# Two graph layers on one core: no idle products at the start, layer 0's last norm behind the first turned blocks of layer 1, and another order at the end

## The chip, the cores and the metric

The kernel runs on one core of a Trainium2 chip. The metric is the device time of one execution in microseconds (us). Engines are named as the profile does: PE is TensorE's products, PEld its weight loads, DVE is VectorE, ACT is ScalarE, POOL is GpSimd, SP is SyncE, which here only issues DMAs.

## What is computed

`x` is 4096 x 512 in float32 and `adj` 4096 x 4096 in int32, with some 0.8% of ones. Two layers follow each other:

```
# layer 0
keep    = (adj > 0) & (cumsum(adj > 0, axis=1) <= 64)
nb_mean = (keep @ x) / max(keep.sum(1), 1)
xj      = leaky_relu(nb_mean @ W_nb.T + b_nb)          # slope 0.01
xi      = leaky_relu(x @ W_line.T + b_line)
x1      = layernorm(x + xi + where(cnt > 0, xj, 0))
# layer 1
Wh  = x1 @ W + bW
e   = leaky_relu((Wh @ a1 + b1)[:, None] + (Wh @ a2 + b2)[None, :], slope 0.2)
att = softmax(where(adj > 0, e, -9e15), axis=1)
out = layernorm(x1 + att @ Wh)
```

## The kernel before

The 4096 rows are 32 blocks of 128. The order of instructions on each engine is the order in which the program writes them: no scheduler moves anything, so an engine that waits holds up all that is written after it on that engine. The same holds for the DMAs that one engine issues. Tiles come from pools with a fixed number of buffers; a tile that takes over a buffer waits for the last reader of the tile before. The pools of layer 1 lie over memory that layer 0 used, and wait for its last readers in the same way.

**Start (L382 to L394).** W_nb and W_line are loaded, brought into order by a VectorE copy, transposed by TensorE in four parts each (`turn_w`, `turn_by_pe`, L149, L282) and copied from PSUM by ScalarE (L150). `spin(n)` puts n transposes of an identity matrix, which nobody reads, on TensorE: 12 at the start and 2 ahead of each part of W_nb. `fold_w` (L356) multiplies W with a1 and a2 on VectorE.

**Layer 0, first stage.** For each block, two products with W_nb and W_line (L340); y = x W_nb^T is split into `y_hi` and `y_lo`. Beside it, adjacency rows are loaded (L160), thresholded by ScalarE (L167), scanned by VectorE for the limit of 64 neighbours (L179 to L184) and stored as byte codes in DRAM (`code_d`).

**Layer 0, second stage.** For each block i, four groups g of 16 products (L502) sum y over its neighbours. Behind group g, `finish(i - 1, g)` does a quarter of the block before: g = 0 scales and bends (L462, L465), g = 1 adds the block's own part, loaded from `own_d` (L497), and takes the statistics (L469, L117 to L123; the power is POOL's), g = 2 applies the norm (L128) and stores the row in `x1_d` (L476), g = 3 takes two dot products with the rows `wa_row` (L481). After the loop, block 31 is finished by itself.

**Layer 1, first product (L786).** For each of 32 strips s of x1: `load_turned(s)` loads it in four DMAs on SP (L553) into one of four slots of `x1s`, `turn_x1(s)` transposes it on VectorE (L566) into a tile `c` of a pool of two, and four products with W make Wh. `finish_wh(s)` (L575) adds the bias row `bias_w` (tile `res`, loaded on SP at L538) into `bt`, and for each second half also makes four differences of it (L580 to L583), so that the later products need seven instead of eight per pair (Winograd's form of Strassen's scheme). At strips 8 to 15, `mask` (ACT L604, then DVE L607) and `score` (ACT L596) of the first two blocks' weights stand in the same loop, `greatest` and `shift` take the row maximum, and at strips 12 to 19 `weigh` (ACT L649) takes the exponential. At strips 22 and 26, `turn` (L668) and `combine` (L681 to L684) prepare the first two parts of the weights.

The terms e2 and st that the masks and scores need go through DRAM on POOL's queue (L763 to L771), behind layer 0's last block.

**Layer 1, weighted sums (L707).** 16 pairs of blocks, each in four parts k; `consume` makes seven products of each part into four PSUM banks: `where` puts products 1 and 2 into one bank, 4 and 7, 5 and 6 into one each, and 3 by itself. Sums of a pair are put together by `end_low` and `end_top` (L732 to L743) and finished by `end_row` (L748, norm, store L752), during the next pair; for the last pair all of this comes after the loop:

```
order = (1, 2, 4, 7, 5, 6, 3) if q < NP * NT - 1 else (1, 2, 6, 7, 5, 4, 3)
...
end_weights(NT - 1)
end_low(NT - 1)
end_row(NB - 1, nc.scalar)
end_top(NT - 1)
end_row(NB - 2, nc.sync)
```

## Time and profile before

| | us |
|---|---|
| median of 3 runs | 1620.12 |
| the 3 runs | 1619.28 to 1620.49 |
| the profiled execution, time | 1619.29 |
| the profiled execution, span | 1617.5 |
| mean granted TensorE clock in it | 0.996 |

The profile is of one execution, and all its clock times count from the span's start. Its time is 1.79 us more than its span, which is what lies around the span. A line of the timeline gives the start, the duration, the engine, the line of the program, the instruction and its tiles; in brackets stands how long the engine stood idle before it and what ended the idling. The trace lists each float32 product twice, so one strip of L786, which is four products, stands there as x8.

### The profile page before, as it was taken

The numbers are of one execution on the slowest core, as the hardware profiler recorded it, in microseconds if no ns is written. First come the engines' busy times: TensorE is split into PE (matmuls) and PEld (weight loads), VectorE is DVE, ScalarE is ACT, GpSimd is POOL, SyncE is SP. The second block draws the span as 40 slices with busy tenths as digits, with TensorE's granted clock in tenths as the row PEclk, the third lists the DMA queues.
The fourth block names the chain that finished last, engine by engine and source line by source line (L and its number), as shares of the span: only waits on it lengthen the run. The fifth ranks groups of instructions, "written<-read, shape, count | busy, mean of one in ns | idle before, by whom it ended". The sixth has DMA issues, their size and how long they took to land.

```text
span 1617.5 us, 18487 instructions
## 1 busy us (share of the span) xinstructions
PE 1584.3 (98%) x6456; PEld 1220.1 (75%) x6456; DVE 1328.7 (82%) x2183; ACT 902.5 (56%) x1054; POOL 257.7 (16%) x395
## 2 busy tenths in 40 slices
PE   9999999999999999989899999999999999999997
PEld 5444448888888787854358888888888888888886
DVE  4999987999999999847787778788888788788763
ACT  2655556677676766413337555567555567555520
POOL 4455532222222221120000000000000000000000
PEclk9999999999999999999999999999999999999999
DMA  8887878767776876352311111111111111111100
GB/s 194 282 260 240 260 210 241 217 196 210 220 212 194 217 205 187 92 130 79 92 46 27 53 40 53 40 27 53 53 40 53 40 28 52 53 40 53 40 7 33
DMA packets 168205, 192.74 MB, mean 119 GB/s; under 512 B 101376, under 2 KB 134176, under 8 KB 159920
## 3 DMA queue, kind: packets, MB, share of 16 engines
q1 hardware_dynamic: 147968, 131.51, 30.1%
q0 software_dynamic: 19712, 59.27, 10.7%
q8 instruction: 50, 0.82, 0.2%
q10 hardware_dynamic: 432, 0.79, 0.1%
q14 instruction: 43, 0.35, 0.1%
HBM read 132.65 MB, written 42.08 MB: 108 GB/s over the span
## 4 chain that ended last, share of the span: by engine, by line
PE 70%; DVE 20%; DMA 4%; issue 3%; ACT 2%; POOL 1%; SPq 0%; POOLq 0%; DVEq 0%; ACTq 0%
PE acc L707 34%; PE pt L707 14%; PE acc L340 9%; PE acc L502 9%; DVE left L179 8%; PE acc L786 4%; DVE left L184 2%; DVE junk L481 2%; DMA a<-in_adj_dram 1%; DVE st L117 1%; DVE own L469 1%; DMA late<-in_x_dram 1%; DVE t L465 1%; DVE t L462 1%; POOL rs L123 1%
## 5 line engine op out<-in xcount | busy, mean ns | idle before, releaser
L502 PE MATMUL acc<-y_hi,kt 128*128 128x512 f32 x1016 | 396.0, 390 | 3.1 <-ACT kt L249 3.1
L502 PE MATMUL acc<-y_lo,kt 128*128 128x512 f32 x1016 | 395.3, 389 | 0.0
L707 PE MATMUL acc<-bt,s 128*128 128x256 f32 x1536 | 342.3, 379 | 0.0
L707 PEld LDWEIGHTS acc<-bt,s 128*128 128x128 f32 x1536 | 291.8, 190 | 39.7
L604 ACT ACTIVATE w<-nat,far 128x1024 f32<-128x1024 uint8 x128 | 136.9, 1135 | 291.6 <-DVE a L668 238.9
L123 POOL TENSOR_TENSOR rs<-ve,neg_half 128x1 f32<-128x1 f32 x64 | 76.0, 1187 | 1026.5 <-DVE ve L121 1026.5
L707 PE MATMUL acc<-bt,a 128*128 128x256 f32 x1024 | 231.6, 379 | 0.0
L707 PE MATMUL pt<-bt,a 128*128 128x256 f32 x1024 | 231.5, 379 | 0.0
L502 PEld LDWEIGHTS acc<-y_hi,kt 128*128 128x128 f32 x1016 | 190.7, 188 | 44.9 <-ACT kt L249 5.3
L502 PEld LDWEIGHTS acc<-y_lo,kt 128*128 128x128 f32 x1016 | 190.7, 188 | 39.4
L707 PEld LDWEIGHTS pt<-bt,a 128*128 128x128 f32 x1024 | 194.6, 190 | 26.9 <-issue 0.5
L707 PEld LDWEIGHTS acc<-bt,a 128*128 128x128 f32 x1024 | 194.6, 190 | 26.5
L668 DVE STREAM_TRANSPOSE a<-w 128x1024 f32<-128x1024 f32 x128 | 153.0, 1225 | 59.4 <-ACT w L649 52.7
L167 ACT ACTIVATE edge<-a,steep 128x2048 bf16<-128x2048 int32 x64 | 127.9, 1998 | 104.5 <-DVE left L184 82.4
L249 ACT ACTIVATE kt<-ktb,steep 128x1024 fp32r<-128x1024 uint8 x124 | 139.4, 1147 | 82.0 <-PE acc L502 64.9
L596 ACT ACTIVATE w<-w,st_n 128x1024 f32<-128x1024 f32 x128 | 149.4, 1233 | 50.7 <-DVE m L607 50.7
L607 DVE CUSTOM_DVE_ANT_0 w<-e_n,w 128x1024 f32<-128x1024 f32 x128 | 149.5, 1221 | 4.3 <-ACT w L604 2.9
L649 ACT ACTIVATE w<-w,nm 128x1024 f32<-128x1024 f32 x128 | 145.4, 1137 | 11.3 <-DVE nm L640 11.3
L179 DVE TENSOR_TENSOR_SCAN left<-two,edge 128x2048 bf16<-128x2048 f32 x32 | 141.3, 4417 | 12.0 <-ACT edge L167 10.9
L179 DVE TENSOR_TENSOR_SCAN left<-two,ends,edge 128x2048 bf16<-128x2048 f32 x32 | 143.2, 4476 | 0.0
L786 PE MATMUL acc<-w,c 128*128 128x512 f32 x256 | 113.6, 602 | 14.9 <-DVE c L566 14.9
L202 ACT CAST code<-left 128x2048 uint8<-128x2048 bf16 x64 | 120.6, 1884 | 7.6 <-DVE left L184 7.6
(114 smaller groups left out, 1529.3 us busy)
## 6 DMA issues: line engine op xcount, KB each, us to landing
a<-in_adj_dram SPq DMA_DIRECT2D x64, 1024.0 KB, 6.0
code_d<-code POOLq DMA_DIRECT2D x64, 256.0 KB, 5.3
nat<-code_d SPq DMA_DIRECT2D x256, 64.0 KB, 2.0
own_d<-xb POOLq DMA_DIRECT2D x32, 256.0 KB, 6.0
own<-own_d SPq DMA_DIRECT2D x32, 256.0 KB, 2.7
x_d<-own POOLq DMA_DIRECT2D x32, 256.0 KB, 2.6
w<-x_d SPq DMA_DIRECT2D x128, 64.0 KB, 2.0
res<-x_d SPq DMA_DIRECT2D x32, 256.0 KB, 2.8
```

What stands on the lines that cost most here:

```text
L167: nc.scalar.activation(edge_of[s], loaded.pop(s), AF.Sigmoid, bias=steep[:, 0:1], scale=STEEP, accum_out=cnts[:, h, b : b + 1],)
L179: nc.vector.tensor_tensor_scan(left, two.to_broadcast([P, CH]), e, NEIGHBORS + 2.0 if h == 0 else end, ALU.max, ALU.subtract,)
L249: nc.scalar.activation(kts[s], bytes_.rearrange("p t (i r) -> p t r i", r=2), AF.Sigmoid, bias=steep[:, 1:2], scale=STEEP,)
L340: nc.tensor.matmul(pl, lhs_t[:, k, :], w_t[name][:, k, :], start=(k == 0), stop=(k == NC - 1),)
L502: nc.tensor.matmul(accs[i], kt[:, k // 2, k % 2, :], term[:, j, :], start=(j == 0 and term is y_hi), stop=(j == NB - 1 and term is y_lo),)
L596: nc.scalar.activation(dst, src, AF.Prelu, bias=bias, scale=scale, alpha=0.2)
L604: nc.scalar.activation(w_i, nats[b, i // 2].bitcast(U8)[:, i % 2, :], AF.Relu, bias=far, scale=-FAR)
L607: nc.vector.tensor_tensor_reduce(w_i, e2_n, w_i, 1.0, -3e38, ALU.subtract, ALU.max, m4s[b][:, i : i + 1])
L649: nc.scalar.activation(w_i, w_i, AF.Exp, bias=nms[b][:, i : i + 1], accum_out=z4s[g][:, r, i : i + 1])
L668: nc.vector.transpose(a[:, r].rearrange("p s (i a) -> p i s a", a=SQ), wts[2 * g + r][:, :, ts(k, 8 * SQ)].rearrange("p i (s x) -> p i s x ...
L707: nc.tensor.matmul(banks[g][n], lhs[:, j, :], bt[:, 4 * k + j, rhs, :], start=(k == 0 and j == 0 and n == mate[0]), stop=(k == NP - 1 and ...
L786: nc.tensor.matmul(pws[s], x1t[:, m, :], ws[:, m, :], start=(m == 0), stop=(m == NC - 1))
```

## The change

- The two identity transposes ahead of each part of W_nb are left out. The 12 at the start stay.
- `late` (three rows: `wa_row` and `bias_nb`, and before them the loaded strips of x) becomes three tiles of a pool `rows` of three buffers, which stays open for layer 1. The turned strips of x1 from the fourth on, `top` and `low`, and the residual rows of even blocks come from `rows` too; the pools `c` and the second `res` buffer go. Five small constants become one tile.
- The second tile of the pool `l1_w`, `early`, is taken right after `front`. The first three turned strips, block 31's own row and its scratch tiles lie in it, and later the first block's weights.
- Block 31's four finishing steps move from the end of layer 0 behind the loads of strips 0 to 3, the load of its own row, the loads for the first masks, and the turns of strips 0 to 2 with the loads of strips 4 to 6. In the loop, strip s + 3 is turned where s + 2 was, and s + 7 loaded.
- The four differences of `bt` are taken from `finish_wh` into `combine_wh`, which is called for one set at a time from strip 16 on, except at 22 and 26, and for what is left in the first part of the weighted sums.
- In the last part the products come in the order 4, 1, 2, 6, 7, 5, 3, and the last pair's sums and norms are written out: the upper block is scaled and its statistics taken in two halves, and it is stored in two halves on two queues.

```diff
-            turn_w("nb", 2)
+            turn_w("nb")
...
+    rows = ctx.enter_context(tc.tile_pool(name="rows", bufs=3, reuse_waits="tile"))
+    late = [rows.tile([P, C], F32, name="c") for _ in range(3)]
+    wa_rows, bias_nb = late[0:2], late[2]
...
-                nc.gpsimd.dma_start(
-                    wa_row.rearrange("p k c -> p (k c)"),
-                    wa_d.rearrange("k c -> (k c)").partition_broadcast(P),
-                )
+                for k in range(2):
+                    nc.gpsimd.dma_start(wa_rows[k], wa_d[k].partition_broadcast(P))
...
+        spare = []
+        def place(name, bufs=2):
+            if spare:
+                return spare.pop(0)
+            return work.tile([P, C], F32, name=name, bufs=bufs)
...
             if g == 2:
-                owns[i] = work.tile([P, C], F32, name="own")
-                nc.sync.dma_start(owns[i], own_d[i])
+                if i < NB - 1:
+                    owns[i] = place("own")
+                    nc.sync.dma_start(owns[i], own_d[i])
...
-        for g in range(NS):
-            finish(NB - 1, g)
...
     front = wp.tile([P, NI, NS * SQ], F32, name="w")
+    early = wp.tile([P, NI, NS * SQ], F32, name="w")
+    spare += [early[:, i, C:] for i in (0, 2, 3)]
+    owns[NB - 1] = early[:, 1, C:]
...
-    bias_w = ep.tile([P, C], F32, name="res")
+    bias_w = ep.tile([P, C], F32, name="res", bufs=1)
     nc.sync.dma_start(bias_w, b_w.partition_broadcast(P))
...
     def turn_x1(s):
         if s < NS:
-            x1ts[s] = ep.tile([P, C], F32, name="c").rearrange("p (m i) -> p m i", i=P)
+            t = early[:, s, :C] if s < 3 else rows.tile([P, C], F32, name="c")
+            x1ts[s] = t.rearrange("p (m i) -> p m i", i=P)
...
         if h == 1:
+            later.append(kk)
+    later = []
+    def combine_wh():
+        if later:
+            b = bt[:, later.pop(0)]
             nc.vector.tensor_tensor(b[:, 4], b[:, 1], b[:, 0], ALU.subtract)
             nc.vector.tensor_tensor(b[:, 5], b[:, 3], b[:, 4], ALU.subtract)
             nc.vector.tensor_tensor(b[:, 6], b[:, 5], b[:, 2], ALU.subtract)
             nc.vector.tensor_tensor(b[:, 1], b[:, 3], b[:, 1], ALU.subtract)
...
-            wts[b] = wp.tile([P, NI, NS * SQ], F32, name="w")
+            wts[b] = early if b == 0 else wp.tile([P, NI, NS * SQ], F32, name="w")
...
-        order = (1, 2, 4, 7, 5, 6, 3) if q < NP * NT - 1 else (1, 2, 6, 7, 5, 4, 3)
+        order = (1, 2, 4, 7, 5, 6, 3) if q < NP * NT - 1 else (4, 1, 2, 6, 7, 5, 3)
...
-            x1rows[b] = ep.tile([P, C], F32, name="res")
+            if b % 2:
+                x1rows[b] = ep.tile([P, C], F32, name="res", bufs=1)
+            else:
+                x1rows[b] = rows.tile([P, C], F32, name="c")
...
+    for s in range(4):
+        load_turned(s)
+    nc.sync.dma_start(owns[NB - 1], own_d[NB - 1])
+    load_nat(0, 0)
+    load_nat(0, 1)
+    for s in range(3):
+        turn_x1(s)
+        load_turned(s + 4)
+    for g in range(4):
+        finish(NB - 1, g)
...
-    for s in range(4):
-        load_turned(s)
-    load_nat(0, 0)
-    load_nat(0, 1)
-    turn_x1(0)
-    turn_x1(1)
     for s in range(NS):
-        if s > 0:
-            load_turned(s + 3)
...
-        turn_x1(s + 2)
+        turn_x1(s + 3)
+        load_turned(s + 7)
...
+        elif s >= FIRST + 8:
+            combine_wh()
...
+        while q == 0 and later:
+            combine_wh()
...
+        if q == NP * NT - 1:
+            end_weights(g)
...
-    end_weights(NT - 1)
-    end_low(NT - 1)
-    end_row(NB - 1, nc.scalar)
-    end_top(NT - 1)
-    end_row(NB - 2, nc.sync)
+    p, rz = banks[NT - 1], rzs[NT - 1]
+    top, low = (rows.tile([P, 2, HC], F32, name="c") for _ in range(2))
+    x_top, x_low = x1rows[NB - 2].rearrange("p (h c) -> p h c", h=2), x1rows[NB - 1]
+    stt = nc.vector.scalar_tensor_tensor
+    st = stat.tile([P, 2, nc.vector.BN_STATS_DIM], F32, name="st2", bufs=1)
+    nc.scalar.copy(top[:, 0], p[1])
+    tt(top[:, 1], top[:, 0], p[6], ALU.add)
+    tt(top[:, 0], top[:, 0], p[2], ALU.add)
+    tt(low[:, 0], top[:, 1], p[7], ALU.add)
+    stt(top[:, 0], top[:, 0], rz[:, 0:1], x_top[:, 0], ALU.mult, ALU.add)
+    nc.vector.bn_stats(st[:, 0], top[:, 0])
+    tt(low[:, 1], low[:, 0], p[5], ALU.add)
+    tt(low[:, 0], low[:, 0], p[4], ALU.subtract)
+    y_low = low.rearrange("p h c -> p (h c)")
+    stt(y_low, y_low, rz[:, 1:2], x_low, ALU.mult, ALU.add)
+    low_stats = ln_stats(y_low)
+    tt(top[:, 1], top[:, 1], p[5], ALU.add)
+    stt(top[:, 1], top[:, 1], rz[:, 0:1], x_top[:, 1], ALU.mult, ALU.add)
+    stt(top[:, 1], p[3], rz[:, 0:1], top[:, 1], ALU.mult, ALU.add)
+    nc.vector.bn_stats(st[:, 1], top[:, 1])
+    mv, rs = ln_rs(st)
+    ln_apply(y_low, low_stats)
+    nc.scalar.dma_start(out_blk(NB - 1), y_low)
+    for h in range(2):
+        ln_apply(top[:, h], (mv, rs))
+        (nc.sync, nc.scalar)[h].dma_start(out_blk(NB - 2)[:, ts(h, HC)], top[:, h])
```

## The prediction, made before the changed kernel ran

> **What bounds the kernel now.** The page's table of engines first: TensorE is busy nearly throughout, so an edit elsewhere counts only where TensorE stands still.
>
> ```profile
> PE 1584.3 (98%) x6456; PEld 1220.1 (75%) x6456; DVE 1328.7 (82%) x2183; ACT 902.5 (56%) x1054; POOL 257.7 (16%) x395
> ```
>
> Then TensorE's own waits (columns: total us, times, longest):
>
> ```profile
> PE acc L786 <- DVE c L566: 14.9, 8, 7.7
> PE acc L502 <- ACT kt L249: 3.1, 4, 1.8
> PE acc L340 <- DVE xt L294: 1.8, 2, 1.0
> ```
>
> The waits for L566, the turned x1 blocks of layer 1's first product (L786), are three quarters of what TensorE loses inside the span. In the chain of waits L707 stands without a break from 834 to 1605 us, so what is won or lost before 834 us reaches the end. TensorE's timeline shows where the 14.9 us lie:
>
> ```profile
> 705.27 0.39 PE L502 MATMUL acc<-y_lo,kt 128*128 128x512 f32 x1
> 713.38 53.33 PE L786 MATMUL acc<-w,c 128*128 128x512 f32 x120 [7.72 <-DVE c L566]
> 768.28 3.70 PE L786 MATMUL acc<-w,c 128*128 128x512 f32 x8 [1.58 <-DVE c L566]
> 772.95 3.70 PE L786 MATMUL acc<-w,c 128*128 128x512 f32 x8 [0.97 <-DVE c L566]
> 777.66 3.70 PE L786 MATMUL acc<-w,c 128*128 128x512 f32 x8 [1.01 <-DVE c L566]
> 782.37 3.70 PE L786 MATMUL acc<-w,c 128*128 128x512 f32 x8 [1.01 <-DVE c L566]
> 786.72 20.87 PE L786 MATMUL acc<-w,c 128*128 128x512 f32 x48 [0.65 <-DVE c L566]
> 809.36 14.00 PE L786 MATMUL acc<-w,c 128*128 128x512 f32 x32 [1.77 <-DVE c L566]
> ```
>
> 7.7 us lie at the seam of the layers, the rest in products 15 to 29 of 32. An undisturbed product takes 3.43 us (VectorE's turns of x1, released by its end, are 3.43 us apart from 718.67 to 722.11); each restart costs some 0.1 us more. The seam in SyncE's timeline:
>
> ```profile
> 705.46 0.35 SPq L538 DMA_DIRECT2D res<-in_L_gnn_bW_dram  x1
> 705.86 7.74 SPq L553 DMA_DIRECT2D w<-x_d  x16
> 713.64 6.12 SPq L591 DMA_DIRECT2D nat<-code_d  x8
> ```
>
> Everything on SyncE's queue stands behind the load of bias_w (`res`), which waits for the last product on y_hi at 705.4. The x1 loads therefore start at 705.86, one per 0.46 us. Later the loop between ScalarE and VectorE sets the pace:
>
> ```profile
> 767.68 1.13 ACT L604 ACTIVATE w<-nat,far 128x1024 f32<-128x1024 uint8 x1
> 770.12 1.24 ACT L596 ACTIVATE w<-w,st_n 128x1024 f32<-128x1024 f32 x1 [1.30 <-DVE m L607]
> 771.26 1.13 ACT L649 ACTIVATE w<-w,nm 128x1024 f32<-128x1024 f32 x1
> 772.39 1.13 ACT L604 ACTIVATE w<-nat,far 128x1024 f32<-128x1024 uint8 x1
> ```
>
> L604, VectorE's L607 (1.23 us), L596, L649, L604 again: 772.39 − 767.68 = 4.71 us a round, against 3.43 for a product. The clock (the number after the five busy times) in half-microsecond stretches:
>
> ```profile
> 709.00:709.50 0.50, 0.00 (x0) 0.00 (x0) 0.10 (x1) 0.00 (x0) 0.25 (x1) 1.00 0.60 174
> 712.00:712.50 0.50, 0.00 (x0) 0.00 (x0) 0.46 (x4) 0.06 (x1) 0.00 (x0) 0.50 1.01 329
> 717.00:717.50 0.50, 0.50 (x2) 0.19 (x1) 0.00 (x0) 0.00 (x0) 0.00 (x0) 1.00 0.48 58
> ```
>
> It is 0.50 from 709.7 to 716.5. Last, the tail:
>
> ```profile
> 1604.30 0.42 DVE L733 TENSOR_TENSOR c<-c,acc 128x256 f32<-128x256 f32 x1 [17.76 <-PE acc L707]
> 1613.70 0.55 DVE L128 TENSOR_SCALAR c<-c,mv,rs 128x512 f32<-128x512 f32 x1 [0.73 <-POOL rs L123]
> 1614.28 0.34 SPq L752 DMA_DIRECT2D out_dram<-c  x1
> ```
>
> **The change part by part.** The sum is made against the profiled execution: 1617.5 us of span and 1.79 around it, 1619.29, which is 0.83 below the median of 1620.12 and at the fast end of the runs.
>
> **1. Spins between the parts of W_nb.** Eight identity transposes of 0.21 us go: 1.7 us of TensorE's queue, up to 1.3 us at the first L340 product (11.26). VectorE's copy (0.43) and ScalarE's (0.59) both fit under a part's four slow transposes (0.87), so TensorE stays busy from 4.8 to about 9.1 anyway. [...] The row: transposes were 0.21 us apart up to 9.75 and 0.13 us after. By the row alone the gain is 1.3 us; [...] Neither reaches the end: TensorE waits for VectorE's turned x again at 56.67 (0.75 us) and 85.48 (1.04 us), and VectorE is there behind the first adjacency load, issued at 24.75 after the fold of the attention vectors, which waits for the row a1 landing at 18.34. I enter 0; [...]
>
> **2. The seam.** The three turns now precede the norm of block 31 as if the products could follow layer 0 without a gap. They cannot. `early` lies in the third buffer, over y_hi's first blocks, and `res` still waits for the last y_hi product and still stands ahead of the x1 loads. The turns wait for loads that start at 705.86 as before. Their fourth pieces are issued at 707.3, 709.2 and 711.1 and, at the 2.7, 2.2 and 2.3 us to landing of these very issues in the trace, land at 710.0, 711.4 and 713.4. With 0.71 us a turn the first product starts at 710.8 instead of 713.38, and the third turn ends at 714.1. Three products take it to 721.1 at full clock.
>
> What pays is the norm, queued behind these turns. It starts at 714.1 instead of 705.70; its two first steps end at 715.6; its `own` row is now issued on SyncE after 16 x1 loads, at 713.64, and lands 2.7 us later (the median of that load) at 716.4. From there the old steps from 707.21 to 712.62 follow, 5.4 us: 721.9, then the fourth turn, 722.6. So product 3 cannot start before 722.65. On POOL, block 31's row and the loads of e2_n and st_n go 9.4 us later: the last of them, issued at 724.4 and 4.6 us under way (median), comes at 738.5 instead of 729. Score 8 asks for it at about 745.5. Covered by 7 us.
>
> The clock: the first product took 713.38 to 718.5, 5.1 us, as half of it ran at 0.50; 1.6 us lost. If the clock is 0.50 until 716.5 again, a product started at 710.8 loses 2.85 and product 3 starts at 723.95. [...] I take 723.3, between the two. Before it was 725.3 (718.5 and two products). Gain 2.0 us.
>
> **3. Look-ahead and late combinations.** The turned blocks have three buffers instead of two, and turn s+3 is made where turn s+2 was; the four subtractions on `bt` (1.58 us) leave products 5 to 16, one set following each product from 16 on, except at 22 and 26. Up to the shift at product 12 the ScalarE/VectorE loop just runs 2.0 us earlier: nm at 763.2 instead of 765.25. It keeps its 4.71 us, and part of the subtractions was hidden in it. What changes is which block each round turns. Turn 16 ends at 764.5 and 17, 18, 19 follow at 769.2, 773.9, 778.7 (before: 15 to 18 at 768.2, 772.9, 777.6, 782.3). TensorE wants 15 to 19 at 764.5, 767.9, 771.4, 774.8 and 778.2: one wait of 0.5 us instead of four. Product 20 needs turn 20, which comes after greatest (1.64), the lm and nm steps (1.35), one set of subtractions (1.58), one eviction (0.60) and itself (0.70): 784.6, a wait of 2.4. Before, product 20 started at 786.72 + 3.54 = 790.2. Gain 5.6 us, the 2.0 included.
>
> From there VectorE needs 0.60 + 0.63 + 1.58 = 2.8 us a product against 3.43, and gains on TensorE except at 22 and 26, where turning and combining a weight part takes 5.0: product 30 may wait 0.5 us. The end is 784.6 + 12 × 3.43 + 0.5 + 0.3 for restarts = 826.6, instead of 834.0. Gain 7.4 us in all.
>
> The last two sets come in the first weights part. VectorE, free at about 831, then has four masks (4.6), greatest to nm (3.1), two sets (3.2), and a turn with its combination (5.5): 847.4. The third part of products needs it at 826.6 + 24.2 = 850.8. 3.4 us to spare: L707 stays without a gap.
>
> **4. The tail.** The order 4, 1, 2, 6, 7, 5, 3 closes the bank of 4 and 7 before that of 5 and 6. VectorE's first sum waits for the latter: 5 ends one product (1.73 us) later than before, so the sum starts at 1604.30 + 1.73 = 1606.0. From there I add steps at their old pitch (0.34 to 0.48 for 256 elements; 256-element forms of the scaled sum and of the statistics, not in the trace, at 0.48, the 512 form less the 0.27 between L681 and L733): last statistics aggregated at 1612.9, with POOL's 0.9 the first half is scaled at 1613.8 and the second is issued at 1614.35. Before: 1614.28. Two transfers of half the size on two queues may land sooner; bounds −0.6 (two waits on POOL to one and a shorter transfer) to +0.4 (three transfers in flight). I take −0.2, near the equal issue times.
>
> **5. The rest.** `late`, x1's turned blocks, top, low and half of the residual rows share one pool of three; a residual row waits for the same read as before (the row step of the pair before), 36 us ahead of use. One more broadcast on POOL (0.55 us) falls in its idle time. 0.
>
> Sum: 7.4 + 0.2 = 7.6, 1619.29 − 7.6 = **1611.7 us**. Against the median the gain would be 8.4: its other runs lost up to 1 us more, perhaps to the clock at the seam.
>
> **The rivals.**
> A. Only the seam gains. If the third buffer comes free no earlier, or the ScalarE/VectorE loop itself must end before product 20, products 15 to 20 keep their waits. For: the loop keeps its 4.71 us. Against: turn 15 now stands ahead of the round that delayed it. 2.0 + 0.2: 1617.1 us. Chance 0.11.
> B. More than I count: the clock is never halved at the seam, TensorE's waits at 56.67 and 85.48 do not eat part 1, and the tail wins 0.6. For: the spread of the runs. Against: part 1's adjacency chain. 0.7 + 1.3 + 0.4 on top: 1609.3. Chance 0.12.
> C. Slower. The norm of block 31 is late, and e2_n and st_n wait behind it: their small pieces meet the x1 loads on the DMA engines (landing took 4.1 to 7.2 us at 713 to 726). Mask and score 8 hold all later turns. Free up to 7 us, then a microsecond each; slower than before from 15. At 20 us: 1611.7 + 13 = 1624.7. Against: twice the longest landing would still be covered. Chance 0.04.
>
> **How the numbers follow.** My forecast has 0.73. About 0.2% (3.2 us) is what a measurement here can tell from no change. Faster is the forecast and B, and a sliver of A: 0.86; same is the rest of A, 0.10; slower is C, 0.04. The forecast's own range is 1610 to 1614: −1 for the clock and the tail, +2 for restarts and DMA waits I did not see. For 8 in 10 I go from 1609.2, near B, to 1615.6, short of A.
>
> **What would show it.** TensorE's gap at the seam near 5.1 us, not 7.7 and not 0; the fourth turn at about 722; no wait at products 15 to 18, one of 2 to 3 us at product 20; the first weights product at 826 to 827; L707 without gaps; the last output as long after TensorE's end as before. The prediction is wrong if the seam's gap closes fully, if products 15 to 18 still wait, or if L707 shows waits in its first three parts.

## The result and the profile after

The changed kernel takes 1612.62 us (median of 6 runs, 1611.52 to 1614.06) beside 1620.3 us before (6 runs, 1619.28 to 1622.26): a ratio of 0.9951, 95% interval 0.9938 to 0.9964, 7.7 us less by the medians and about 7.9 by the ratio. The forecast was 1611.7. The profiled execution took 1612.2 us, with a span of 1610.4; all numbers of "after" below are from it.

In the changed kernel L509 is what L502 was (layer 0's products), L809 is L786 (layer 1's first product), L575 turn_x1, L724 is L707 (the products by the weights).

The page's table of engines: TensorE is as busy as before, in a span 7.1 us shorter.

```profile
PE 1583.4 (98%) x6448; PEld 1219.1 (76%) x6448; DVE 1328.3 (82%) x2186; ACT 903.2 (56%) x1054; POOL 258.2 (16%) x396
```

TensorE's waits (total us, times, longest): those for the turned x1 blocks were 14.9 us in 8 places and are 8.0 in 3. The block of the seam now carries the name `w`, as the first three turned blocks lie in `early`.

```profile
PE acc L809 <- DVE w L575: 5.4, 1, 5.4
PE acc L509 <- ACT kt L249: 2.9, 4, 1.8
PE acc L809 <- DVE c L575: 2.6, 2, 2.2
PE acc L340 <- DVE xt L294: 1.7, 2, 1.1
```

The same places in TensorE's timeline (start, duration, instructions, idle time before in brackets):

```profile
704.41 0.39 PE L509 MATMUL acc<-y_lo,kt 128*128 128x512 f32 x1
710.20 13.47 PE L809 MATMUL acc<-w 128*128 128x512 f32 x24 [5.40 <-DVE w L575]
723.51 55.10 PE L809 MATMUL acc<-w,c 128*128 128x512 f32 x128
778.95 3.70 PE L809 MATMUL acc<-w,c 128*128 128x512 f32 x8 [0.34 <-DVE c L575]
784.88 41.88 PE L809 MATMUL acc<-w,c 128*128 128x512 f32 x96 [2.23 <-DVE c L575]
826.60 3.62 PE L724 MATMUL pt<-bt,a 128*128 128x256 f32 x16
```

The seam's gap is 5.4 us. Products 0 to 2 take 13.3 us (710.20 to 723.51) where three undisturbed ones take 10.3. Products 3 to 18 run through; 19 waits 0.34 us, 20 waits 2.23, and after it nothing. The weights stage starts at 826.60 instead of 833.96.

SyncE's queue at the seam: the load of bias_w still stands ahead of the x1 loads and still goes out only when layer 0 ends; the `own` row of block 31 now comes behind 16 x1 loads.

```profile
704.61 0.35 SPq L546 DMA_DIRECT2D res<-in_L_gnn_bW_dram  x1
705.00 7.56 SPq L561 DMA_DIRECT2D w<-x_d  x16
712.65 0.38 SPq L777 DMA_DIRECT2D w<-own_d  x1
```

The clock (the number after the five busy times) in half-microseconds:

```profile
709.00:709.50 0.50, 0.00 (x0) 0.00 (x0) 0.06 (x1) 0.00 (x0) 0.00 (x0) 0.74 0.43 123
715.50:716.00 0.50, 0.50 (x2) 0.32 (x1) 0.37 (x1) 0.00 (x0) 0.00 (x0) 0.50 0.65 201
716.00:716.50 0.50, 0.50 (x2) 0.19 (x1) 0.47 (x2) 0.00 (x0) 0.00 (x0) 0.93 0.42 135
```

By the shares of the first and the last of these rows it falls at 709.2 and comes back at 716.1, so products 0 to 2 run 5.9 of their 13.3 us at half speed. And the tail: first sum, the upper row's statistics put together, POOL's `rs`, the two halves scaled, last issue.

```profile
1598.67 0.42 DVE L877 TENSOR_TENSOR c<-c,acc 128x256 f32<-128x256 f32 x1 [19.48 <-PE acc L724]
1605.37 0.21 DVE L122 BATCH_NORM_AGGREGATE mv<-st 128x2 f32<-128x12 f32 x1
1605.91 0.71 POOL L126 TENSOR_TENSOR rs<-ve,few 128x1 f32<-128x1 f32 x1 [1.76 <-DVE ve L124]
1606.66 0.74 DVE L131 TENSOR_SCALAR c<-c,mv,rs 128x256 f32<-128x256 f32 x2 [0.44 <-POOL rs L126]
1607.42 0.35 ACTq L896 DMA_DIRECT2D out_dram<-c  x1
```

TensorE ends at 1600.31; the last output is issued 7.11 us later (before: 6.62), and the span ends 10.09 us later (before: 9.84).

### The profile page after: what moved, and what is told of

The parts are those of the page before. It is cut to its first block, busy times and chain, and to the rows that moved or that the text cites. A ratio compares the mean times of both kernels' runs of the same rounds, so it can differ in the third digit from the quotient of the medians.

```text
span 1610.4 us, 18487 instructions
## 1 busy us (share of the span) xinstructions
PE 1583.4 (98%) x6448; PEld 1219.1 (76%) x6448; DVE 1328.3 (82%) x2186; ACT 903.2 (56%) x1054; POOL 258.2 (16%) x396
## 4 chain that ended last, share of the span: by engine, by line
PE 69%; DVE 23%; DMA 3%; issue 2%; ACT 1%; POOL 1%; SPq 0%; DVEq 0%; POOLq 0%; ACTq 0%
PE acc L724 34%; PE pt L724 14%; DVE left L179 10%; PE acc L340 9%; PE acc L509 9%; PE acc L809 3%; DVE left L184 2%; DVE junk L487 2%; DVE own L475 1%; DVE st L117 1%; DVE t L471 1%; DMA a<-in_adj_dram 1%; DVE t L468 1%; DVE own L131 1%; DVE c L575 1%
## 5 line engine op out<-in xcount | busy, mean ns | idle before, releaser
L509 PE MATMUL acc<-y_hi,kt 128*128 128x512 f32 x1016 | 395.8, 390 | 2.9 <-ACT kt L249 2.9
L509 PE MATMUL acc<-y_lo,kt 128*128 128x512 f32 x1016 | 395.3, 389 | 0.0
L724 PE MATMUL acc<-bt,s 128*128 128x256 f32 x1536 | 342.1, 379 | 0.0
L724 PEld LDWEIGHTS acc<-bt,s 128*128 128x128 f32 x1536 | 291.8, 190 | 39.7
L621 ACT ACTIVATE w<-nat,few 128x1024 f32<-128x1024 uint8 x128 | 136.9, 1135 | 277.1 <-DVE a L685 237.0
L126 POOL TENSOR_TENSOR rs<-ve,few 128x1 f32<-128x1 f32 x64 | 76.1, 1190 | 1020.5 <-DVE ve L124 1020.5
L724 PE MATMUL acc<-bt,a 128*128 128x256 f32 x1024 | 231.6, 379 | 0.0
L724 PE MATMUL pt<-bt,a 128*128 128x256 f32 x1024 | 231.5, 379 | 0.0
L509 PEld LDWEIGHTS acc<-y_hi,kt 128*128 128x128 f32 x1016 | 190.7, 188 | 44.4 <-ACT kt L249 4.8
L509 PEld LDWEIGHTS acc<-y_lo,kt 128*128 128x128 f32 x1016 | 190.7, 188 | 39.5
L724 PEld LDWEIGHTS pt<-bt,a 128*128 128x128 f32 x1024 | 194.6, 190 | 26.9 <-issue 0.5
L724 PEld LDWEIGHTS acc<-bt,a 128*128 128x128 f32 x1024 | 194.6, 190 | 26.5
L249 ACT ACTIVATE kt<-ktb,few 128x1024 fp32r<-128x1024 uint8 x124 | 139.8, 1147 | 84.7 <-PE acc L509 67.8
L167 ACT ACTIVATE edge<-a,few 128x2048 bf16<-128x2048 int32 x64 | 127.9, 1998 | 100.5 <-DVE left L184 78.3
L624 DVE CUSTOM_DVE_ANT_0 w<-e_n,w 128x1024 f32<-128x1024 f32 x128 | 149.5, 1221 | 9.1 <-ACT w L621 7.7
L179 DVE TENSOR_TENSOR_SCAN left<-few,edge 128x2048 bf16<-128x2048 f32 x32 | 141.3, 4417 | 12.4 <-ACT edge L167 11.3
L179 DVE TENSOR_TENSOR_SCAN left<-few,ends,edge 128x2048 bf16<-128x2048 f32 x32 | 143.2, 4476 | 0.0
L340 PE MATMUL acc<-wt_nb,xt 128*128 128x512 f32 x256 | 115.5, 594 | 2.5 <-DVE xt L294 1.7
```

Source lines behind the costliest of these rows:

```text
L167: nc.scalar.activation(edge_of[s], loaded.pop(s), AF.Sigmoid, bias=steep[:, 0:1], scale=STEEP, accum_out=cnts[:, h, b : b + 1],)
L179: nc.vector.tensor_tensor_scan(left, two.to_broadcast([P, CH]), e, NEIGHBORS + 2.0 if h == 0 else end, ALU.max, ALU.subtract,)
L249: nc.scalar.activation(kts[s], bytes_.rearrange("p t (i r) -> p t r i", r=2), AF.Sigmoid, bias=steep[:, 1:2], scale=STEEP,)
L340: nc.tensor.matmul(pl, lhs_t[:, k, :], w_t[name][:, k, :], start=(k == 0), stop=(k == NC - 1),)
L509: nc.tensor.matmul(accs[i], kt[:, k // 2, k % 2, :], term[:, j, :], start=(j == 0 and term is y_hi), stop=(j == NB - 1 and term is y_lo),)
L621: nc.scalar.activation(w_i, nats[b, i // 2].bitcast(U8)[:, i % 2, :], AF.Relu, bias=far, scale=-FAR)
```

## The experiments

Layer 0's last product ended at anything from 704.8 to 708.8 us in the fourteen traces of this study, with code ahead of it that differs in the spins and in where some tiles lie. A stretch that starts there is therefore a cleaner measure of the seam and of layer 1's first products than a total. The table has two stretches: from the end of layer 0 to the first product by the weights, and the part of it from product 3 on. (The trace of before merges products 0 to 14; product 3 is put at 725.4 there, as in the prediction.) Each is read from one trace. From product 3 on, kernels with the same loop agree within 0.1 us (103.1 or 103.2 in five), apart from m_warm; from layer 0's end to product 3 the seven traces with the changed seam scatter from 17.9 to 18.7 us. The ratio is to the kernel before, run on the same chip alongside it, with its 95% interval. Where an edit adds lines, the line numbers of that kernel's rows are a few off from the changed kernel's.

| kernel | layer 0's end | end to weights stage, us | product 3 to weights stage, us | ratio of times |
|---|---|---|---|---|
| before | 705.66 | 128.3 | 108.6 | 1 |
| changed | 704.80 | 121.8 | 103.1 | 0.9951 [0.9938, 0.9964] |
| a_spins | 705.98 | 128.5 | - | 0.9998 [0.9990, 1.0006] |
| b_old_tail | 705.66 | 121.1 | 103.1 | 0.9947 [0.9935, 0.9960] |
| c_early_sets | 707.47 | 121.1 | 102.7 | 0.9947 [0.9935, 0.9960] |
| d_ahead_2 | 704.93 | 121.8 | 103.8 | 0.9958 [0.9944, 0.9972] |
| h_seam_only | 706.01 | 123.7 | 105.8 | 0.9965 [0.9952, 0.9977] |
| n_two_bufs | 707.72 | 127.1 | 108.6 | 0.9979 [0.9973, 0.9986] |
| m_warm | 708.78 | 122.5 | 104.4 | 0.9954 [0.9941, 0.9968] |
| o_warm_20 | 707.40 | 122.0 | 103.1 | 0.9952 [0.9938, 0.9966] |
| e_bias_behind | 706.10 | 114.4 | 103.2 | 0.9904 [0.9889, 0.9918] |
| f_bias_slot | 706.89 | 114.1 | 103.2 | 0.9905 [0.9890, 0.9919] |
| k_mask_first | 706.23 | 118.8 | 100.2 | 0.9924 [0.9909, 0.9939] |
| l_all | 704.88 | 110.4 | 100.2 | 0.9878 [0.9864, 0.9891] |

### a_spins: the spins alone

```diff
-            turn_w("nb", 2)
+            turn_w("nb")
```

(in the kernel before, as the change has it)

> The kernel before with one edit of the change alone: no spins between the parts of W_nb. What is open: in the changed kernel's trace the last product of layer 0 ended 0.86 us earlier than before (704.8 against 705.66), which the prediction did not have. Theory (the prediction's part 1): the spins' time is eaten by the next wait for the turned x, the seam comes at 705.7 as before, the total is that of before within 0.3 us (ratio 1.0000). Rival (the spins are worth their time): the first L340 product comes at 10.5 instead of 11.3, layer 0 ends about 0.9 us earlier and the total falls by 0.9 us (ratio 0.9994).

Measured: no difference (1620.36 us beside 1620.40). The trace of this run shows why a gain of 0.8 us at the first product is not to be had for certain. TensorE's timeline, this kernel first, then the changed one:

```profile
5.29 4.70 PE L149 MATMUL pt<-ident,t 128*128 128x128 f32 x20 [1.10 <-DVE t L282]
10.67 5.42 PE L340 MATMUL acc<-wt_nb,xt 128*128 128x512 f32 x8 [0.68 <-ACT wt_nb L150]
```
```profile
5.28 4.53 PE L149 MATMUL pt<-ident,t 128*128 128x128 f32 x20 [1.09 <-DVE t L282]
10.49 3.70 PE L340 MATMUL acc<-wt_nb,xt 128*128 128x512 f32 x8 [0.68 <-ACT wt_nb L150]
```

The first four products of L340 (x8) come at 10.67 and 10.49 instead of 11.26, but here they take 5.42 us where they take 3.70 in the other. Of the thirteen traces of kernels without the spins, three (a_spins, f_bias_slot, k_mask_first) show 5.4 to 5.6 us at this place, ten 3.70. So the 0.6 to 0.8 us gained at the first product in these two (0.4 to 1.9 over the thirteen, beside the one trace with spins) are paid back in about one execution of four. And the 0.86 us by which layer 0 ended earlier in the changed kernel's profile is not shown to be a gain of the spins: its end scatters by 4.0 us over the traces.

### b_old_tail: the tail alone undone

```diff
-        if q == NP * NT - 1:
-            end_weights(g)
-        order = (1, 2, 4, 7, 5, 6, 3) if q < NP * NT - 1 else (4, 1, 2, 6, 7, 5, 3)
+        order = (1, 2, 4, 7, 5, 6, 3) if q < NP * NT - 1 else (1, 2, 6, 7, 5, 4, 3)
...
+    end_weights(NT - 1)
+    end_low(NT - 1)
+    end_row(NB - 1, nc.scalar)
+    end_top(NT - 1)
+    end_row(NB - 2, nc.sync)
```

(and the new tail left out)

> The changed kernel with the tail of before: last pair's products in the order 1, 2, 6, 7, 5, 4, 3 and each row normed whole. Theory (from the traces: the span ends 10.09 us after TensorE's last product in the changed kernel, 9.84 before): the new tail loses a little, so this kernel is 0.25 us faster than the changed one, 1612.4 against 1612.6, with the first sum 3.4 us before TensorE's end and the last output issued 6.6 us after it. Rival (the prediction's part 4): the new tail gains 0.2 us, so this one is 0.2 us slower. Second rival: the two half-size outputs land sooner in most runs than in the one profiled; then this one is up to 0.6 us slower.

Measured: 1612.79 us, not to be told from the changed kernel by its time (ratios 0.9947 and 0.9951). The traces can tell. VectorE's first sum and SyncE's last issue with the old tail:

```profile
1597.06 0.42 DVE L753 TENSOR_TENSOR c<-c,acc 128x256 f32<-128x256 f32 x1 [17.76 <-PE acc L724]
1607.04 0.34 SPq L772 DMA_DIRECT2D out_dram<-c  x1
```

TensorE ends at 1600.42 in this trace. The first sum starts 3.36 us ahead of that, in the changed kernel 1.64; the last issue is 6.62 us behind it, in the changed kernel 7.11. The span ends 9.9 us behind it instead of 10.1. Over all traces it is 9.8 to 9.9 us in the four with the old tail and 10.0 to 10.5 in the ten with the new one. The new tail costs 0.2 us of span; it gains nothing.

### c_early_sets: look-ahead of three, subtractions made at once

```diff
             later.append(kk)
+            combine_wh()
...
-        elif s >= FIRST + 8:
-            combine_wh()
```

> The changed kernel with the four subtractions on bt made at once, behind the second finish of each pair as before, so that of part 3 only the look-ahead of three turned blocks is left. Theory: the look-ahead brings the gain of this stage and the late sets nothing: the subtractions of products 5 to 16 lie largely beside ScalarE's part of the round, so the shift of product 12 comes at most 1 us later, and in return product 20 has no set of subtractions ahead of it; waits of about 0.8, 1.2 and 0.8 us at products 18, 19 and 20, first weights product at about 826.0, total 0.6 us below the changed kernel (1612.0). Rival (the late sets are what lets the turns come in time): the round up to product 12 is lengthened by the 1.58 us of each of the two sets in it, the waits of products 18 to 20 grow to 3 us and more in sum beyond those of the changed kernel, first weights product at 829.5 or later, total 1615.5 or more.

Measured: 102.7 us from product 3 to the weights stage (0.4 less than the changed kernel), 1612.89 us in all. The theory held: with the look-ahead in place the late sets are worth nothing. Waits of 0.7, 1.0 and 0.7 us at products 18, 19 and 20 take the place of 0.3 and 2.2 at 19 and 20.

### d_ahead_2: look-ahead of two, late sets

```diff
-        turn_x1(s + 3)
-        load_turned(s + 7)
+        if s > 0:
+            turn_x1(s + 2)
+            load_turned(s + 6)
```

> The changed kernel with the look-ahead of before, turn s+2 behind product s, and the late sets kept. Theory (the look-ahead is what gains): products 15 to 19 wait for their turns again by 1 to 2.4 us each, the first weights product comes at about 830.9 and the total is 4.2 us above the changed kernel (1616.8). Rival (the late sets or the seam make the gain): waits and the start of the weights stage as in the changed kernel, 826.6 within 1 us, total within 1 us of it.

The theory fell: 103.8 us from product 3 on, 0.7 above the changed kernel, not 4.2. VectorE's timeline around product 8 shows what the theory had left out. First this kernel, then the changed one:

```profile
740.30 0.69 DVE L584 TENSOR_TENSOR bt<-acc,res 128x512 f32<-128x512 f32 x1 [2.12 <-PE acc L809]
740.91 0.70 DVE L575 STREAM_TRANSPOSE c<-w 128x512 f32<-128x512 f32 x1
741.54 1.18 DVE L624 CUSTOM_DVE_ANT_0 w<-e_n,w 128x1024 f32<-128x1024 f32 x1
```
```profile
740.88 0.71 DVE L575 STREAM_TRANSPOSE c<-w 128x512 f32<-128x512 f32 x1 [2.15 <-PE acc L809]
744.31 0.71 DVE L575 STREAM_TRANSPOSE c<-w 128x512 f32<-128x512 f32 x1 [2.15 <-PE acc L809]
744.94 1.18 DVE L624 CUSTOM_DVE_ANT_0 w<-e_n,w 128x1024 f32<-128x1024 f32 x1
```

With three buffers and turn s+2, the turn's buffer was last read by product s−1, which has ended: the turn at 740.91 waits for nothing and the first mask (L624) follows at once. With turn s+3 the buffer is that of product s itself; the turn at 744.31 waits 2.15 us for it, and the mask stands behind it on VectorE. From product 3 the first mask comes after 18.6 us here and after 21.4 in the changed kernel, as in the kernel before, and with it the whole loop of ScalarE and VectorE. The third buffer can thus be spent in two ways: turns one further ahead, or masks one product earlier. This kernel took the second, and lost 0.7 us by it.

### h_seam_only and n_two_bufs: both halves of part 3 undone

```diff
             later.append(kk)
+            combine_wh()
...
-            t = early[:, s, :C] if s < 3 else rows.tile([P, C], F32, name="c")
+            t = early[:, s, :C] if s < 3 else duo[s % 2]
...
-        turn_x1(s + 3)
-        load_turned(s + 7)
+        if s > 0:
+            turn_x1(s + 2)
+            load_turned(s + 6)
...
-        elif s >= FIRST + 8:
-            combine_wh()
```

(n_two_bufs; `duo` is two tiles of the pool `rows`. In h_seam_only a third tile without a reader or writer was asked for instead, after every second turn.)

> The changed kernel with both halves of part 3 undone: turn s+2 behind product s into two alternating buffers (so that it waits for product s again), and the four subtractions made at once. Seam and tail stay as changed. Why: with three buffers and turn s+2 (d_ahead_2) the turn waits for no product, the first mask comes 3.4 us earlier (741.54 instead of 744.94) and the gain survives another way, so that run took away less than it was meant to. Theory (the seam is worth 2 us, part 3 the other 5): from product 3 at about 723.5 on the waits are those of before, 108.6 us to the first weights product (725.4 to 834.0 before), which comes at 832.1; total 1618.1, 5.5 above the changed kernel. Rival (the waits of products 15 to 20 go away with the seam alone): first weights product within 2 us of 826.6, total 1614.5 at most.

Measured: 105.8 us from product 3 on. The edit did not do what it was meant to: the turns did not wait for product s, as with three buffers, so the tile that nothing writes seems to have got no place. The run is thus d_ahead_2 with early sets, and shows that without the longer look-ahead the late sets do count, by 2.0 us (105.8 against 103.8). The run as meant:

> What h_seam_only was meant to be: turn s+2 behind product s into two fixed tiles used in turn, so that it waits for product s to end as before, and the four subtractions made at once; seam and tail as changed. (In h_seam_only the third tile was never written and got no place, so the turns went through three buffers and did not wait for product s.) Theory (third buffer or late sets are both needed for nothing else than to keep turns and masks from queueing behind product s): from product 3 on as before, 108.6 us to the first weights product, waits at products 15 to 18, 20 or 21 and 27; first weights product at 832.2 with product 3 at 723.6, total 5.5 us above the changed kernel, 2 below before. Rival (h_seam_only's 105.8 us is what the seam alone gives): 105.8 us again, 829.5, total 2.7 us above the changed kernel.

Measured: 108.6 us, as before and as expected. TensorE's timeline has the waits of before again:

```profile
726.20 41.36 PE L811 MATMUL acc<-w,c 128*128 128x512 f32 x96
769.14 3.70 PE L811 MATMUL acc<-w,c 128*128 128x512 f32 x8 [1.58 <-DVE c L576]
773.80 3.70 PE L811 MATMUL acc<-w,c 128*128 128x512 f32 x8 [0.96 <-DVE c L576]
778.51 3.70 PE L811 MATMUL acc<-w,c 128*128 128x512 f32 x8 [1.01 <-DVE c L576]
783.23 3.70 PE L811 MATMUL acc<-w,c 128*128 128x512 f32 x8 [1.02 <-DVE c L576]
```

The seam, the spins and the tail together bring 0.9979 [0.9973, 0.9986], that is 3.4 us (2.3 to 4.4). In the traces the stretch from layer 0's end to the weights stage is 1.2 us shorter; where the other 2 us of the medians lie, no run here shows (the profiled execution of before, 1619.29, is itself 2.5 below the median of the runs of before that n_two_bufs is compared with, 1621.82). From product 3 on, the 5.5 us between this kernel and the changed one are part 3's. By the two ratios part 3 is worth 4.5 us give or take 2.4 us (estimate), which does not contradict the traces.

### m_warm and o_warm_20: products that keep the clock up

```diff
+    warm = ps_acc.tile([P, C], F32, name="acc")
+    for _ in range(36):
+        nc.tensor.matmul(warm[:, :P], ws[:, 0, :P], ws[:, 0, :P], start=True, stop=True)
```

> The changed kernel with 36 products of 128x128 on W between the layers, into a PSUM tile that nobody reads, so that TensorE is busy in the seam's gap; they add nothing to the output. It measures what the halved clock costs there. Theory: 36 products take about 4.7 us of the 5.4 us gap; the clock stays at 1.00, products 0 to 2 take 10.3 us instead of 13.3, product 3 waits for the fourth turn alone and starts at about 721.7 instead of 723.5, total 1.9 us below the changed kernel (1610.7). Rival (the norm of block 31 and the round of ScalarE and VectorE set the later waits, not TensorE's clock): product 3 earlier but the waits at products 19 and 20 grow by as much, total within 0.5 us of the changed kernel.

Measured: 1614.58 us, no gain. The 36 products took 8.2 us and held up product 0 themselves; the clock stayed at 1.00, the first three products took 10.3 us, and product 3 came at 726.96, 18.2 us behind layer 0's end, as without them. (Its 104.4 us from there on contain a halving at product 20, 1.3 us.) The same with 20:

> m_warm with 20 useless products on W instead of 36. In m_warm the 36 took 8.2 us, not the 4.7 that were reckoned (two passes of 0.114 us each), and held up product 0 themselves until 716.7, so it did not measure the clock. 20 take 4.6 us and end ahead of the first turn. Theory (the halved clock costs what lies between the end of the fourth turn and product 3, 1.9 us in the changed kernel's trace: 721.61 to 723.51): clock 1.00 throughout, products 0 to 2 take 10.4 us, product 3 starts within 0.3 us of the end of the fourth turn, about 16.9 us after layer 0 ends instead of 18.7; total 1.8 us below the changed kernel (ratio to the kernel before 0.9940). Rival (the wait at product 20 grows instead, or the clock is halved later, as at product 20 in m_warm): ratio within 0.0004 of the changed kernel's 0.9951.

Measured: ratio 0.9952, the rival's answer. The 20 products ended at 711.86, product 0 could start only at 714.18, as the x1 loads were slower in this trace (16 issues in 8.76 us instead of 7.56), and the clock was halved all the same, after an idle stretch of 2.3 us:

```profile
707.24 4.62 PE L807 MATMUL acc<-w 128*128 128x128 f32 x40
714.18 12.26 PE L813 MATMUL acc<-w 128*128 128x512 f32 x24 [2.32 <-DVE w L575]
726.29 55.10 PE L813 MATMUL acc<-w,c 128*128 128x512 f32 x128
```
```profile
714.00:715.00 1.00, 0.81 (x2) 0.49 (x3) 0.81 (x2) 0.00 (x0) 0.00 (x0) 1.00 0.47 124
716.00:717.00 1.00, 1.00 (x3) 0.47 (x2) 0.90 (x2) 0.00 (x0) 0.00 (x0) 0.50 0.49 132
```

What the clock costs in the total was not settled by these two. In the seven traces with the changed seam product 3 starts 0.5 to 1.9 us after the fourth turn has ended, 1.2 on average; the changed kernel's 1.9 is the most, h_seam_only's 0.5 the least. Where the clock was halved later (o_warm_20) it is 0.9 us, with the clock up (m_warm) 0.3 us. By these the halved clock costs 0.2 to 1.6 us (estimate).

### e_bias_behind and f_bias_slot: what holds the seam's loads

```diff
-    nc.sync.dma_start(bias_w, b_w.partition_broadcast(P))
...
     for s in range(4):
         load_turned(s)
+    nc.sync.dma_start(bias_w, b_w.partition_broadcast(P))
     nc.sync.dma_start(owns[NB - 1], own_d[NB - 1])
```

f_bias_slot has this and a tile allocated ahead of `early`, which takes the place over y_hi:

```diff
+    second = wp.tile([P, NI, NS * SQ], F32, name="w")
     early = wp.tile([P, NI, NS * SQ], F32, name="w")
...
+    nc.gpsimd.memset(second[:, 0, 0:1], 0.0)
...
-            wts[b] = early if b == 0 else wp.tile([P, NI, NS * SQ], F32, name="w")
+            wts[b] = (early, second)[b] if b < 2 else wp.tile([P, NI, NS * SQ], F32, name="w")
```

> The changed kernel with the load of bias_w moved on SyncE's queue behind the first 16 x1 loads, nothing else. Theory (the queue makes the seam's gap, as the prediction's part 2 says): the x1 loads are done before layer 0 ends; turn 0 then waits only for the last y_hi product, as `early` lies over y_hi; gap about 0.9 us instead of 5.4, clock never halved, product 3 starts at about 716.5 instead of 723.5, total 6.8 us below the changed kernel (1605.8). Rival (the norm of block 31 or the landing of the loads sets the seam): the gap shrinks but product 3 waits for the norm, total 1610 or more.

Measured: 1606.03 us, expected 1605.8. TensorE's timeline at the seam:

```profile
706.73 10.57 PE L809 MATMUL acc<-w 128*128 128x512 f32 x24 [0.64 <-DVE w L574]
717.31 55.20 PE L809 MATMUL acc<-w,c 128*128 128x512 f32 x128
820.50 3.62 PE L723 MATMUL pt<-bt,a 128*128 128x256 f32 x16
```

The gap is 0.64 us instead of 5.4, the three first products take 10.6 us, and from product 3 on all goes as in the changed kernel (103.2 us), 7.4 us earlier when both are counted from layer 0's end. One DMA's place in a queue was worth about as much as the whole change. (The changed kernel's trace has the latest product 3 of the seven; beside the others the gain is 6.7 to 7.3 us. The ratios give 7.6.)

> As e_bias_behind, and `early` takes another of the three buffers (a second tile is allocated ahead of it, over y_hi), so that turns 0 to 2 wait for their loads alone. Theory: no gap at the seam, 0.8 us less than e_bias_behind (1605.0). Rival (turn 0 waits for something else that ends with layer 0): time and gap of e_bias_behind.

Measured: no gap at all at product 0 (last product of layer 0 at 706.50, product 0 at 706.73), but product 3 waits 0.59 us for the fourth turn, behind the norm of block 31, whose `own` row is issued behind bias_w at 707.14. From layer 0's end it gains 0.3 us on e_bias_behind, not 0.8; the ratios do not part the two.

### k_mask_first: masks ahead of the waiting turn

```diff
-        turn_x1(s + 3)
-        load_turned(s + 7)
         if FIRST <= s < FIRST + 8:
             b, i = divmod(s - FIRST, NI)
             mask(b, i)
             score(b, i)
+        if s in (FIRST + 4, FIRST + 8):
+            greatest((s - FIRST - 4) // NI)
+        turn_x1(s + 3)
+        load_turned(s + 7)
...
-                greatest(b)
```

> The changed kernel with the masks of products 8 to 15 (and the reductions `greatest` of products 12 and 16) written ahead of turn_x1(s + 3) instead of behind it, so that on VectorE no mask stands behind a turn that waits for product s to end. Theory (from d_ahead_2: the loop of ScalarE and VectorE is late because its first mask is queued behind a waiting turn): first mask at 741.5 instead of 744.9, shift of the first mask block at 760.0 instead of 763.4, turns 16 to 20 at about 765, 770, 774, 777 and 781, each just in time, no wait above 0.3 us at products 15 to 20; first weights product at 823.2 instead of 826.6, total 3.4 us below the changed kernel (1609.2). Rival (the turns come late behind the masks): waits of 0.5 to 1.5 us at products 16 to 19 take the place of those at 19 and 20, total within 1 us of the changed kernel or above it.

Measured: 1609.87 us, ratio 0.9924; 100.2 us from product 3 on, 2.9 less than the changed kernel (expected 3.4). TensorE's timeline:

```profile
724.76 51.66 PE L809 MATMUL acc<-w,c 128*128 128x512 f32 x120
776.77 48.38 PE L809 MATMUL acc<-w,c 128*128 128x512 f32 x112 [0.35 <-DVE c L575]
824.99 3.62 PE L724 MATMUL pt<-bt,a 128*128 128x256 f32 x16
```

And VectorE's first mask:

```profile
743.34 1.20 DVE L624 CUSTOM_DVE_ANT_0 w<-e_n,w 128x1024 f32<-128x1024 f32 x1
```

One wait of 0.35 us is left of products 3 to 31. The first mask comes 18.6 us after product 3, as in d_ahead_2, and the turns are three ahead as in the changed kernel: both uses of the third buffer at once.

### l_all: the three together

The diffs of f_bias_slot, k_mask_first and b_old_tail on the changed kernel, with the two loads of f_bias_slot in this order:

```diff
     for s in range(4):
         load_turned(s)
     nc.sync.dma_start(owns[NB - 1], own_d[NB - 1])
+    nc.sync.dma_start(bias_w, b_w.partition_broadcast(P))
```

> What the runs point to, together, on the changed kernel: the load of bias_w and the third buffer as in f_bias_slot, with the `own` row of block 31 loaded ahead of bias_w, the masks ahead of the turns as in k_mask_first, and the tail of before as in b_old_tail. Theory (the three gains lie one behind the other on TensorE's path and add): layer 0 ends at about 705.8, product 3 starts 10.5 us later without a wait, 100.2 us from product 3 to the first weights product as in k_mask_first, which comes at 816.5; total 1602 us, 10 to 11 below the changed kernel. Rival (with TensorE earlier, VectorE's backlog of masks and sets reaches the third weights part): L724 waits there, total 1604 or more.

Measured: 1601.21 us (1600.58 to 1603.40), ratio 0.9878: 20 us below the kernel before, some 12 below the changed one. TensorE's timeline:

```profile
704.72 10.46 PE L811 MATMUL acc<-w 128*128 128x512 f32 x24
715.01 51.66 PE L811 MATMUL acc<-w,c 128*128 128x512 f32 x120
767.02 48.38 PE L811 MATMUL acc<-w,c 128*128 128x512 f32 x112 [0.35 <-DVE c L576]
815.25 3.62 PE L725 MATMUL pt<-bt,a 128*128 128x256 f32 x16
```

Product 0 follows the last product of layer 0 (704.49) without a gap, product 3 comes 10.1 us after layer 0's end, and from there 100.2 us, as in k_mask_first. The products by the weights show no wait: the rival did not come.

## Why the prediction was right

**The sum.** 7.6 us were forecast against the profiled execution, 7.1 were measured (spans 1617.5 and 1610.4): 0.86 because layer 0 ended earlier in this one execution, 6.5 from there to the weights stage (1.0 at the seam, 5.5 behind it), less 0.25 at the tail. The first of these is scatter that the prediction did not count on. Without it 6.2 would have been left, so that the sum came so near is in part luck: the scatter stood in for two terms that came out smaller, the seam and the tail. The 6.5 us lie where TensorE stood still ahead of 834 us, as was read from its waits, and L724 has no wait. How the gain divides is read from the traces; the ratios put more of it outside part 3 (3.4 us in n_two_bufs, of which the traces show 1.0), and that stays open.

**1. Spins.** Entered at 0; a_spins gives 0.9998. The traces show a gain and a loss: the first product comes earlier by 0.4 to 1.9 us, and in three of thirteen traces 1.7 to 1.9 us are lost in it. In a_spins the clock column stands at 1.00 from 10 to 16 us while the four products take 5.42 us instead of 3.70; what slows them, no run here shows. The cover that was named is there: TensorE waits again for VectorE's turned x at 48.87 and 57.10 us, 1.7 us in all.

**2. The seam.** Right: bias_w's load and `early`'s place hold the x1 loads, so that the gap shrinks to 5.4 us and does not close; e_bias_behind and f_bias_slot show these two as its cause, the first worth 7.4 us and the second 0.3 in their traces. Right also: the fourth turn, behind the norm of block 31, ended 16.8 us after layer 0 (at 721.61); 17.0 had been worked out. Mis-sized was the clock. The prediction put product 3 at 17.6 us after layer 0's end, about midway between its own 17.0 (never halved) and 18.3 (halved), by the author's estimate. In all seven traces with a gap of 5.1 to 5.6 us it was halved, 3.0 to 4.4 us after the gap began, and product 3 came 17.9 to 18.7 us after layer 0's end, 18.3 on average: the halved case as it had been worked out. The changed kernel's own trace has the latest, 18.7 (before: 19.7), so in it the seam brought 1.0 us and not 2.0; on the average of the seven it is 1.4. The cover of e2_n and st_n held: their last issue ended at 733.6, and ScalarE's first score, at 746.17, was released by VectorE.

**3. Look-ahead and late sets.** From product 3 to the weights stage 103.3 us were forecast (826.6 less 723.3) and 103.1 measured, 5.5 less than before. The waits are those forecast: none at products 15 to 18, 0.34 at 19 (0.5), 2.23 at 20 (2.4); turns 16 to 19 end at 764.8, 769.5, 774.2 and 778.9 (764.5, 769.2, 773.9, 778.7), with product 3 0.2 us later than forecast. The 0.5 us allowed at product 30 did not come. What the prediction did not see is that the parts of this step replace each other. From product 3: none of them 108.6 (n_two_bufs), the third buffer alone 105.8 (h_seam_only), with late sets 103.8 (d_ahead_2), with the longer look-ahead 102.7 (c_early_sets), with both 103.1. Nor did it see that with the look-ahead of three the first mask still stands behind a turn that waits for product s, as it did before; k_mask_first shows that this costs 2.9 us.

**4. The tail.** Wrong in sign: −0.2 forecast, +0.25 in the profiles of before and after (the medians do not tell the two tails apart). The first sum (1.64 us ahead of TensorE's end) and the last aggregation (5.06 to 5.27 us behind it) came where they had been put. Mis-sized is what follows: 1.08 us from the aggregation to the first scaling for 0.9, with POOL's `rs` at 0.71 instead of 0.55, and 0.76 from there to the last issue for 0.55, as the two halves are scaled 0.37 us apart. With the smaller transfers the span ends a little sooner after the last issue (3.0 us, 3.2 before), which does not make up for the 0.49 that the issue came later.

**Rivals.** A, that only the seam gains, is what n_two_bufs was built to be; it keeps its waits, and the changed kernel does not. B asked for a clock that is never halved at the seam; it was halved in every trace with that gap. C did not come: no score or turn behind product 8 was released by a load of e2_n or st_n.

## What to carry to other kernels

When an engine's queue holds a wait, ask what stands behind it and does not need it: here the masks behind a turn, the x1 loads behind bias_w. With these two moved, `early` in another buffer and the `own` row ahead of bias_w (l_all), the stretch from layer 0's end to the weights stage is 11 us shorter than in the changed kernel, which itself had won 6.5 on the kernel before. Parts of one change can replace each other (a further buffer, a longer look-ahead, work put off), so try each with the others absent as well as present. Where a kernel's start scatters by microseconds, measure a stage from its own beginning.

## What was not expected of the hardware

The prediction reckoned with an idle stretch halving TensorE's clock only at the seam, where it put the gap at 5.1 us. In three traces the clock was halved after an idle stretch of 1.9 to 2.3 us. The same place in two traces, e_bias_behind first, then n_two_bufs, and the clock of the first:

```profile
50.24 5.40 PE L340 MATMUL acc<-wt_nb,xt 128*128 128x512 f32 x8 [1.91 <-DVE xt L294]
49.96 3.70 PE L340 MATMUL acc<-wt_nb,xt 128*128 128x512 f32 x8 [1.93 <-DVE xt L294]
```
```profile
50.00:51.00 1.00, 0.76 (x2) 0.30 (x3) 1.00 (x3) 0.29 (x1) 0.00 (x0) 0.77 0.92 385
53.00:54.00 1.00, 1.00 (x2) 0.38 (x2) 1.00 (x1) 1.00 (x1) 0.00 (x0) 0.52 1.05 254
```

The clock was halved after 1.91 us in e_bias_behind (from 50.54 to 53.96: four products in 5.40 us instead of 3.70), after 2.23 us in m_warm (at product 20, from 788.4 to 791.8) and after 2.32 us in o_warm_20 (from 715.1 to 718.5); 1.93 us in n_two_bufs (four products in 3.70 us) and 2.23 us ahead of 784.88 in the changed kernel (clock 1.00 from 780 to 790) were not followed by a halving. Each of the three halvings lasted 3.4 us; those behind the seam's gaps of 5.1 to 7.7 us lasted 6.8. Idle stretches of the same length were thus followed by a halving in one execution and by none in another; what decides it, no run here shows.

POOL's `rs` (128x1) of the upper row took 0.71 us with the new tail (the changed kernel, c_early_sets and d_ahead_2), where it starts while VectorE is scaling a row of 512, and 0.55 us in the four traces with the old tail (before, a_spins, b_old_tail, l_all), with VectorE idle. In b_old_tail:

```profile
1605.88 0.55 POOL L126 TENSOR_TENSOR rs<-ve,few 128x1 f32<-128x1 f32 x1 [2.98 <-DVE ve L124]
```

VectorE was busy beside a short `rs` too: the lower row's in the changed kernel took 0.56 us (at 1603.59) beside two sums of VectorE. The scaling ran for 0.3 us more when the upper row's `rs` began (1605.68 + 0.54 against 1605.91), and 0.16 us were lost; what makes it longer was not tried. It bears on the tail's order: the changed one scales the lower row while the upper row's `rs` runs.
